# Attention scores in four 64x64 tiles of the array instead of two 64x128 tiles

## The chip, the cores and the metric

The kernel runs on one core of a Trainium2 chip. The metric is the device time of one execution in microseconds (us). Engines are named as in the profile: PE is TensorE (PEld its weight loads), DVE is VectorE, ACT is ScalarE, POOL is GpSimd and SP is SyncE, which here only issues DMAs.

## What is computed

The input is a batch of 16 images with 384 channels of 32 x 32 pixels. Two layers follow each other, each with a group normalisation (32 groups) before it and a residual after it: attention over the 1024 pixels of an image with 8 heads of 48 channels, and a depthwise convolution of 7 x 7. Cut to what matters:

```python
qkv = jnp.einsum('bnc,oc->bno', xt, w_qkv)
qkv = qkv.reshape(b, n, 3, NUM_HEADS, HEAD_DIM).transpose(2, 0, 3, 1, 4)
q, k, v = (qkv[0], qkv[1], qkv[2])
attn = jnp.einsum('bhnd,bhmd->bhnm', q, k) * SCALE
attn = jax.nn.softmax(attn, axis=-1)
out = jnp.einsum('bhnm,bhmd->bhnd', attn, v)
...
x = x + _L0_conv_ref(_gn(x), L0_conv_w_qkv, L0_conv_w_proj, L0_conv_b_proj)
x = x + _L1_conv_ref(_gn(x), L1_conv_weight)
```

All of it is in fp32.

## The kernel before, in words

The eight heads of an image are taken in four pairs, so there are 16 x 4 = 64 pairs, numbered u. A tile qks[u] holds the queries (index 0) and keys (index 1) of one pair for all 1024 pixels, with the channels on partitions: head 0 of the pair on partitions 0 to 47, head 1 on 64 to 111.

The scores of a pair are computed in 16 steps: two halves h of 512 queries, and in each of them eight blocks i of 128 keys. One step, s_step (L487), takes a score buffer in PSUM of 128 partitions (keys) x 2 heads x 512 queries, which is one PSUM bank for each head. It fills it with one product per head j: the stationary operand lhsT is 48 channels x 128 keys, the moving operand rhs 48 channels x 512 queries. The two heads lie on different rows of the array. Then ACT takes the exponential of the whole buffer into an SBUF tile e (L501). There are 16 x 64 = 1024 steps.

av_step (L503) multiplies the values with e: for each head a product with 128 keys x 64 columns as stationary operand (48 channels, a column of ones whose product is the sum of the softmax, and columns that aren't used) and 128 keys x 512 queries as moving operand. It accumulates over the eight blocks of keys into one PSUM bank, head 0 on partitions 0 to 63, head 1 on 64 to 127. take (L517) copies the bank out.

PSUM has three buffers of two banks that scores, queries and keys, values and projection share (ps_s), and two buffers of one bank (ps_o) for the accumulators. A score step therefore has to wait until the exponential three steps back has read its buffer.

The order of the work is written out by the program: the loop at the end of run() takes eight score steps in a row, then eight value steps (SIZES = [8] * 8, so an image has eight such groups), and between them the other stages for PE: queries and keys (qk_step, L435), values (v_step, L463) and the projection (proj_step, L555). A planner with estimated costs (clock for PE, vclock for DVE) decides where DVE's instructions stand: catch_up puts the taps of the depthwise convolution of an earlier image there (conv_tap, L636), and functions with a due time (after) such as divide, which divides by the softmax sums. act_slot does the same for ACT. The order of each engine's instructions is thus fixed when the program is built.

The convolution of three of the 48 channel tiles (128 channels of an image) is computed on PE at the end (conv_on_pe, L739): for each tap four products side by side, each with 128 rows x 32 columns of the array.

Of the kernel before, what the change touches and what calls it, by code (L numbers as in the profile page):

```python
# [16 lines left out]
P = 128  # L17
# [27 lines left out]
def kernel(  # L45
# [25 lines left out]
    nc = tc.nc  # L71
# [7 lines left out]
    HALF = N // 2  # L79
# [30 lines left out]
    def run(general):  # L110
        tag = "g" if general else "f"
        with ExitStack() as stack:
# [20 lines left out]
            def psum(name):  # L133
                return ps_s.tile([P, 2, HALF], F32, tag="s", name=name)

            xns, x1s, qks, os_, accs, es, xn1s = {}, {}, {}, {}, {}, {}, {}
# [350 lines left out]
            def s_step(n):  # L487

                u, h, i = n // (2 * NT), n // NT % 2, n % NT
                ps = psum(f"ps_s_{n}")  # L490
                for j in range(2):
                    r = slice(64 * j, 64 * j + D)
                    nc.tensor.matmul(  # L493
                        ps[:, j, :],
                        lhsT=qks[u][r, 1, i * P : (i + 1) * P],
                        rhs=qks[u][r, 0, h * HALF : (h + 1) * HALF],
                        start=True,
                        stop=True,
                    )
                es[n] = epool.tile([P, 2, HALF], F32, tag="e", name=f"e_{n}")  # L500
                nc.scalar.activation(es[n], ps, AF.Exp, scale=SCALE)  # L501

# [808 lines left out]
            for b, n0, size in [  # L1311
                (b, b * PER_B + sum(SIZES[:g]), SIZES[g]) for b in range(B) for g in range(len(SIZES))
            ]:
                r = n0 - b * PER_B
# [5 lines left out]
                for n in range(n0, n0 + size):  # L1320
                    s_step(n)
# [17 lines left out]
                for n in range(n0, n0 + size):  # L1339
                    av_step(n)  # L1340
                    u, h, i = n // (2 * NT), n // NT % 2, n % NT
# [102 lines left out]
```

## Time and profile before

| | us |
|---|---|
| median of 3 runs | 2908.01 (2907.54 to 2911.57) |
| span of the profiled execution, first to last instruction | 2904.5 |
| PE busy | 2894.4 |
| DVE busy | 2565.6 |
| ACT busy | 1461.4 |
| score matmuls (L493), busy | 914.2 |
| value matmuls (L509), busy | 907.2 |

In the rows of the profile a group is named by its line, engine, operation and tiles; "48*128" is the shape of the stationary operand (rows x columns of the array that are used), and "48x512 f32" that of the operand that streams or is loaded. After the shape come the count, the busy time in us (overlapping records counted once), the mean duration in ns, and the idle time of the engine before these instructions with what ended it. A product in fp32 is two weight loads and two matmuls in the records. Matmul records overlap, and a matmul's record is longer than the time by which it delays the next. Rows of a timeline give the start in us, the length in us, the engine, the line, the operation and how many records were merged.

The time around the span is 2908.0 - 2904.5 = 3.5 us. The clock of TensorE was 1.000 of full speed over the span. The DMA queues moved 175.80 MB, at a mean share of the DMA engines between 0 and 7 tenths in slices of 73 us.

### The profile page before, as it was taken

How to read it: one execution, taken by the hardware profiler on the slowest of the kernel's cores; microseconds unless marked ns; L12 is line 12 of the kernel's file. 1: busy time of each engine (PE TensorE's matmuls, PEld its weight loads, DVE VectorE, ACT ScalarE, POOL GpSimd, SP SyncE). 2: the span in 40 equal slices, each digit the busy share in tenths (PEclk: the TensorE clock that was granted, in tenths of full speed). 3: DMA queues.
4: the chain of work that ended last, by engine and by line, in shares of the span. 5: the costliest groups of instructions: out<-in, count | busy, mean ns of one | idle time of the engine just before them, and what ended most of it. 6: DMA issues, size and time to landing. Idle time of an engine off the chain costs nothing.

```text
span 2904.5 us, 30161 instructions
## 1 busy us (share of the span) xinstructions
PE 2894.4 (100%) x11446; PEld 1169.7 (40%) x11446; DVE 2565.6 (88%) x2559; ACT 1461.4 (50%) x1745; POOL 262.0 (9%) x411
## 2 busy tenths in 40 slices
PE   9999999999999999999999999999999999999999
PEld 4343343433434343343433434343343433434333
DVE  5313999989899898998989899898998989899997
ACT  2546445464453645545465454645545455454641
POOL 3111004010100101000010100101001010100101
PEclk9999999999999999999999999999999999999999
DMA  7422022220312203012120212213022130212346
GB/s 287 131 26 63 16 36 77 38 67 23 65 33 43 70 21 84 16 35 70 35 71 16 65 41 43 67 24 84 16 36 70 28 77 16 55 50 43 83 125 174
DMA packets 74284, 175.80 MB, mean 61 GB/s; under 512 B 30528, under 2 KB 32464, under 8 KB 72592
## 3 DMA queue, kind: packets, MB, share of 16 engines
q0 software_dynamic: 34336, 114.90, 15.9%
q1 hardware_dynamic: 38080, 55.20, 7.6%
q10 hardware_dynamic: 1712, 3.67, 0.4%
q8 instruction: 92, 1.51, 0.2%
q14 instruction: 64, 0.52, 0.1%
HBM read 118.61 MB, written 28.72 MB: 51 GB/s over the span
## 4 chain that ended last, share of the span: by engine, by line
PE 100%; DVE 0%; ACT 0%; POOL 0%; issue 0%; POOLq 0%
PE ps_s L493 31%; PE acc L509 31%; PE ps_qk L442 17%; PE ps_v L468 9%; PE ps_proj L562 8%; PE ps_conv L756 2%; PE ps_proj L599 1%; PE warm L1182 0%; PE ps_st_x L332 0%; PE ps_sum L588 0%; ACT qk L449 0%; POOL sc_x L353 0%; DVE x L360 0%; DVE x L777 0%; DVE ones_warm L1176 0%
## 5 line engine op out<-in xcount | busy, mean ns | idle before, releaser
L640 DVE SCALAR_TENSOR_TENSOR x<-xn,wsym,x 128x930 f32<-128x930 f32 (+9 forms) x2170 | 2363.9, 1172 | 138.8 <-ACT xn L364 138.7
L501 ACT ACTIVATE e<-ps_s 128x1024 f32<-128x1024 f32 x1024 | 952.5, 1051 | 54.5 <-PE ps_s L493 51.6
L493 PE MATMUL ps_s<-qk 48*128 48x512 f32 x4096 | 914.2, 596 | 1.1 <-ACT qk L449 1.1
L509 PE MATMUL acc<-e,v 128*64 128x512 f32 x4096 | 907.2, 595 | 0.0
L493 PEld LDWEIGHTS ps_s<-qk 48*128 48x128 f32 x4096 | 376.5, 185 | 535.0 <-ACT e L501 257.2
L509 PEld LDWEIGHTS acc<-e,v 128*64 128x64 f32 x4096 | 283.0, 137 | 608.2 <-issue 599.7
L442 PE MATMUL ps_qk<-x,wqk 128*128 128x512 f32 x1152 | 505.7, 595 | 1.0 <-DVE x L360 1.0
L520 ACT COPY o<-acc 128x512 f32<-128x512 f32 x128 | 75.2, 587 | 602.5 <-PE acc L509 602.3
L442 PEld LDWEIGHTS ps_qk<-x,wqk 128*128 128x128 f32 x1152 | 216.1, 190 | 287.1 <-issue 285.7
L468 PE MATMUL ps_v<-wv,x 128*128 128x384 f32 x768 | 252.0, 488 | 0.0
L562 PE MATMUL ps_proj<-o,wp 128*128 128x512 f32 x540 | 234.2, 592 | 0.0
L449 ACT COPY qk<-ps_qk 128x1024 f32<-128x1024 f32 x96 | 96.8, 1009 | 254.1 <-PE ps_qk L442 254.1
L577 POOL DMA_DIRECT2D x<-in_x x45 | 39.3, 872 | 1796.7 <-ACT x L570 1423.1
L468 PEld LDWEIGHTS ps_v<-wv,x 128*128 128x128 f32 x768 | 144.6, 190 | 109.7 <-ACT e L501 12.1
L562 PEld LDWEIGHTS ps_proj<-o,wp 128*128 128x128 f32 x540 | 102.6, 190 | 126.0 <-issue 120.3
L477 ACT COPY v<-ps_v 128x384 f32<-128x384 f32 x128 | 55.1, 483 | 185.6 <-PE ps_v L468 185.6
L570 ACT ACTIVATE x<-ps_proj,bp 128x1024 f32<-128x1024 f32 x45 | 50.2, 1115 | 182.7 <-PE ps_proj L562 182.7
L545 DVE TENSOR_TENSOR o<-o,inv 128x1024 f32<-128x1024 f32 x63 | 77.4, 1228 | 69.7 <-DMA inv<-inv 52.9
L364 ACT ACTIVATE xn<-x,sc_x 128x1024 f32<-128x1024 f32 x47 | 54.9, 1231 | 71.6 <-DMA sc_x<-gr_x 62.4
L756 PE MATMUL ps_conv<-sh,mat 128*32 128x480 f32 (+3 forms) x656 | 67.8, 569 | 0.0
L387 DVE BATCH_NORM_STATS2 bs_all<-xs 128x6 f32<-128x512 f32 x84 | 52.1, 682 | 17.3 <-DMA xs<-in_x 17.1
L458 POOL DMA_DIRECT2D qk<-qk x96 | 47.3, 526 | 116.4 <-ACT qk L449 115.4
(143 smaller groups left out, 565.4 us busy)
## 6 DMA issues: line engine op xcount, KB each, us to landing
x<-in_x POOLq DMA_DIRECT2D x90, 512.0 KB, 5.6
inv<-inv SPq DMA_DIRECT2D x126, 256.0 KB
out<-x POOLq DMA_DIRECT2D x45, 512.0 KB, 3.8
xs<-in_x POOLq DMA_DIRECT2D x42, 512.0 KB, 6.1
qk<-qk POOLq DMA_DIRECT2D x96, 128.0 KB, 5.9
o<-o SPq DMA_DIRECT2D x90, 64.0 KB
sh<-xd SPq DMA_DIRECT2D x32, 160.0 KB
x<-in_x SPq DMA_DIRECT2D x6, 512.0 KB
```

Of the source, the lines that this page charges most:

```text
L442: nc.tensor.matmul(ps[:, h, :], lhsT=wqk[:, k, s, t, :], rhs=xns[b][:, k, h * HALF : (h + 1) * HALF], start=(k == 0), stop=(k == NK - 1),)
L449: nc.scalar.copy(halves(qks[u][:, s, :]), ps)
L468: nc.tensor.matmul(ps[:, j, 0:C], lhsT=xns[b][:, k, t * P : (t + 1) * P], rhs=wv[:, k, :], start=(k == 0), stop=(k == NK - 1),)
L477: nc.scalar.copy(dst.rearrange("p (h d) -> p h d", d=D + 1)[:, :, 0:D], ps[:, j, 0:C].rearrange("p (h d) -> p h d", d=D),)
L493: nc.tensor.matmul(ps[:, j, :], lhsT=qks[u][r, 1, i * P : (i + 1) * P], rhs=qks[u][r, 0, h * HALF : (h + 1) * HALF], start=True, stop=True,)
L501: nc.scalar.activation(es[n], ps, AF.Exp, scale=SCALE)
L509: nc.tensor.matmul(accs[u, h][64 * j : 64 * j + 64, :], lhsT=v_of(u, i, j), rhs=e[:, j, :], start=(i == 0), stop=(i == NT - 1),)
L520: nc.scalar.copy(os_[u][:, h * HALF : (h + 1) * HALF], accs.pop((u, h)))
L545: nc.vector.tensor_tensor(os_[u], os_[u], invs.pop(u), ALU.mult)
L562: nc.tensor.matmul(ps[:, h, :], lhsT=wp[:, t, o * P : (o + 1) * P], rhs=os_[NP * b + t][:, h * HALF : (h + 1) * HALF], start=(t == 0), sto ...
L640: nc.vector.scalar_tensor_tensor(acc, xn1s[b, k].rearrange("p (h w) -> p h w", w=W)[:, iy, ix], wsym[:, k, dy + PAD, dx + PAD : dx + PAD + 1],
L756: nc.tensor.matmul(dst[CH * i : CH * (i + 1), :].rearrange("p (y x) -> p y x", x=W)[:, :, ox], lhsT=mats[k][:, i, d0 * KS + dx + PAD, :], ...
```

## The change

In s_step each head's product is split in two by keys: c = 0 takes the first 64 of the block's 128 keys and writes to partitions 0 to 63 of the score buffer, c = 1 takes the other 64 and writes to partitions 64 to 127. The queries are the same for both. The four products of a step lie on four different quarters of the array. The buffer, its contents, the exponential that reads it and everything else are as they were.

```diff
                 ps = psum(f"ps_s_{n}")
                 for j in range(2):
                     r = slice(64 * j, 64 * j + D)
-                    nc.tensor.matmul(
-                        ps[:, j, :],
-                        lhsT=qks[u][r, 1, i * P : (i + 1) * P],
-                        rhs=qks[u][r, 0, h * HALF : (h + 1) * HALF],
-                        start=True,
-                        stop=True,
-                    )
+                    for c in range(2):
+                        nc.tensor.matmul(
+                            ps[64 * c : 64 * c + 64, j, :],
+                            lhsT=qks[u][r, 1, i * P + 64 * c : i * P + 64 * c + 64],
+                            rhs=qks[u][r, 0, h * HALF : (h + 1) * HALF],
+                            start=True,
+                            stop=True,
+                        )
```

## The prediction

> **What bounds the kernel now.** I read the engine shares first, then the chain that ended last, then the costliest groups.
>
> ```profile
> PE 2894.4 (100%) x11446; PEld 1169.7 (40%) x11446; DVE 2565.6 (88%) x2559; ACT 1461.4 (50%) x1745; POOL 262.0 (9%) x411
> ...
> PE ps_s L493 31%; PE acc L509 31%; PE ps_qk L442 17%; PE ps_v L468 9%; PE ps_proj L562 8%; PE ps_conv L756 2%; PE ps_proj L599 1%; PE warm L1182 0%; PE ps_st_x L332 0%; PE ps_sum L588 0%; ACT qk L449 0%; POOL sc_x L353 0%; DVE x L360 0%; DVE x L777 0%; DVE ones_warm L1176 0%
> ...
> L501 ACT ACTIVATE e<-ps_s 128x1024 f32<-128x1024 f32 x1024 | 952.5, 1051 | 54.5 <-PE ps_s L493 51.6
> L493 PE MATMUL ps_s<-qk 48*128 48x512 f32 x4096 | 914.2, 596 | 1.1 <-ACT qk L449 1.1
> L509 PE MATMUL acc<-e,v 128*64 128x512 f32 x4096 | 907.2, 595 | 0.0
> L493 PEld LDWEIGHTS ps_s<-qk 48*128 48x128 f32 x4096 | 376.5, 185 | 535.0 <-ACT e L501 257.2
> ...
> L756 PE MATMUL ps_conv<-sh,mat 128*32 128x480 f32 (+3 forms) x656 | 67.8, 569 | 0.0
> ```
>
> PE is busy for the whole span and the chain never leaves it, so a nanosecond won or lost on PE in the score stage is one in the end. The score stage (L493) is 31% of the chain. 4096 matmul records over 1024 steps of two products are four records a step: each fp32 product is two weight loads and two matmuls, called pass a and pass b here. 914.2 us over 1024 steps is 893 ns for four matmuls of 589 ns: they overlap. How they overlap is in the timeline of the weight loads, at the turn into a score group and out of it, and at the start of the convolution on PE, which is the one place with four tiles at once:
>
> ```profile
> 1020.87 0.30 PEld L493 LDWEIGHTS ps_s<-qk 48*128 48x128 f32 x4 [0.76 <-issue]
> 1021.40 0.19 PEld L493 LDWEIGHTS ps_s<-qk 48*128 48x128 f32 x2 [0.23 <-issue]
> 1021.83 0.19 PEld L493 LDWEIGHTS ps_s<-qk 48*128 48x128 f32 x2 [0.23 <-issue]
> ...
> 1026.84 0.33 PEld L493 LDWEIGHTS ps_s<-qk 48*128 48x128 f32 x4 [0.53 <-ACT e L501]
> 1027.93 0.20 PEld L509 LDWEIGHTS acc<-e,v 128*64 128x64 f32 x4 [0.76 <-issue]
> 1028.41 0.14 PEld L509 LDWEIGHTS acc<-e,v 128*64 128x64 f32 x2 [0.28 <-issue]
> 1028.85 0.14 PEld L509 LDWEIGHTS acc<-e,v 128*64 128x64 f32 x2 [0.28 <-issue]
> ...
> 2826.91 0.16 PEld L756 LDWEIGHTS ps_conv<-sh,mat 128*32 128x32 f32 x8 [0.76 <-issue]
> 2827.37 0.13 PEld L756 LDWEIGHTS ps_conv<-sh,mat 128*32 128x32 f32 x4 [0.30 <-issue]
> 2827.80 0.13 PEld L756 LDWEIGHTS ps_conv<-sh,mat 128*32 128x32 f32 x4 [0.30 <-issue]
> ```
>
> A load starts when a matmul of its tile starts, so these rows count slots. In a slot of 0.43 us (1021.83 less 1021.40) all tiles run one pass side by side: two score tiles, two tiles of the second product (L509), four convolution tiles. A score step is two slots, 0.86 us. Three rows of the views by source line give the shortest, median and longest matmul:
>
> ```profile
> L493 PE MATMUL ps_s<-qk x4096: 589/589/693, 27.5 to 2796.5; 48*128 48x512 f32 x196
> L509 PE MATMUL acc<-e,v x4096: 592/592/645, 50.2 to 2814.8; 128*64 128x512 f32 x196
> L756 PE MATMUL ps_conv<-sh,mat x656: 551/565/617, 2826.9 to 2897.4; 128*32 128x480 f32 x48, 128*32 128x496 f32 x48, 128*32 128x464 f32 x47, 128*32 128x512 f32 x21
> ```
>
> The longest are the first of a group, which wait for their weights with nothing to cover the load: 104 ns more than the usual one with 128 columns, 53 with 64, 25 with 32 (617 less the 592 of the same 512 elements on L509). The timeline agrees: the first slot is 0.53 us in a score group and 0.48 in a group of L509.
>
> **What the Trainium skill says.** "TensorEngine Tiling (Array Packing)", Available Configurations, lists 64x64 as four tiles; Key Properties says that tiles work independently and that a change of tiling mode drains TensorE. The trace agrees on the drain: from the last matmul start of one stage (1020.34 of L442, 1027.41 of L493) to the first load of the next it is 0.53 and 0.52 us, against slots of 0.43, some 0.09 for each turn. "TensorE: Matmul & The Clock Gate", section LDWEIGHTS, says that a load takes as long as it has columns, whatever its rows, at 1.2 per ns; the 104, 53 and 25 ns above agree. Part 3 of that page gives 10.6 times for 16 tiles of 32x32, rows and columns split together; no stage of this kernel splits both, so the trace can't confirm it.
>
> **The change, part by part.** Removed from each step: four loads of 128 columns and four matmuls of 512 elements. Added: eight loads of 64 columns and eight matmuls of the same 512 elements, in four tiles. The elements streamed per tile don't change; the number of tiles does.
>
> 1. Steady slots. If four tiles overlap as two do, a step stays two slots of 429 ns: cost 0. What hides the doubled instruction count is the other tiles' streaming. The convolution is the nearest row: four loads and four matmuls a slot, for 45 us without a stop from 2851.8, at 390 to 429 ns a slot for 464 to 512 elements. The new score stage needs the same eight instructions every 429 ns, so issue should hold. The cover gone, each ns on a slot costs 1024 x 2 = 2.05 us.
> 2. First slot of a group. SIZES makes groups of 8 steps, 1024 / 8 = 128 groups. The exposed load shrinks from 128 to 64 columns: 533 to 480 ns, as on L509, a gain of 53 ns. Its bounds are 0 (the two column halves of a row pair load one after the other, two times 53) and 53. I take 53: on L509 two loads of 64 columns lie side by side (0.14 us for x2, each 0.137).
> 3. Skew. Tiles start one after another: x2 of 187 ns takes 0.19 us, x4 of 109 ns takes 0.13, so the last of two starts some 7 ns late and the last of four some 20. A group ends with its last tile, then drains: 14 ns more each. Bounds 0 and 14; I take 14.
> 4. Drain. 0.09 us in and out for all pairs of shapes that occur; I take no change, with 5 ns each way as bound, 2 x 128 x 5 = 1.3 us.
> 5. The wait for the score buffer. The first load of a step waits for the exponential that frees one of three buffers (257.2 us of PEld's idle time, nearly all covered). In the last step of a group that load starts at 1026.84 while the matmul running then began at 1026.55, so it has until 1026.98. Everything later on PE is queued behind it. A load half as long needs 53 ns less there, and the exponential starts 14 ns later: the slack grows. Few slots stall now (some 0.6 us in all, in three groups), so I count 0.
> 6. ACT, DVE, DMA. ACT (50%) has the same exponentials. DVE waits 138.7 us in 15 waits for the normalised next image, some 9 us an image, which depends on PE; PE coming 8 x 39 = 0.3 us earlier per image is absorbed there. No DMA is added or moved, on SP's or POOL's queue either; only 8192 more PE instructions are fetched, at a rate the convolution has already.
>
> Sum: 128 x (53 - 14) = 5.0 us less. The profiled span of 2904.5 becomes 2899.5; the median of the runs is 3.5 us above the span, which I keep: 2908.0 - 5.0 = 2903.0 us.
>
> **The rivals.**
>
> A, the forecast: four tiles overlap, and the short first load pays. With items 2 to 4 at their bounds the gain is 4.0 to 7.0 us: 2901.0 to 2904.0.
>
> B, loads of the two halves follow one another: no gain in item 2, the skew stays, 128 x 14 = 1.8 us more: 2909.8. For it: the two halves read the same 48 partitions, which no two loads of a group do now in a tile of fewer than 128 rows. Against: L509 loads two halves over all rows side by side.
>
> C, the slower side: the two column halves of a row pair stream the same query columns through the same rows, and get in each other's way. Place: every score slot. In full, halves take turns and a step has four slots: 1024 x 2 x 429 ns = 879 us more, some 3782. In part, a few ns on a slot: from 5.3 ns (to make up the 5.0 us and add 5.8) the kernel is slower by more than 0.2%, and at 6.3 ns it is at 2916. For it: no stage here splits rows and columns together, PE has nothing to cover a longer slot, and the convolution's slots carry 2 to 5 ns over their elements at 1.2 per ns. Against: L509 and L756 stream two and four tiles through the same rows without loss, L493 two through different rows.
>
> D, the turn gets cheaper, since L509 next to the scores has the same column split: half of 0.09 us saved on the way in gives 128 x 46 ns = 5.9 us more, 2897.1. Against: the turn costs 0.09 us also from L493 to L468, where only the row split changes.
>
> That the change doesn't do what it says would show as 4096 records on L493; the loop over c makes 8192.
>
> **How the numbers follow.** Differences of 0.2%, 5.8 us, are about what a measurement can tell from none, so the mark for faster is 2902.2, inside A's own range. A has 0.62: 0.29 of it beyond the mark (skew partly hidden, cheaper drain), 0.33 within. B has 0.07, within. D has 0.07, faster. C has 0.24, slower: 0.14 in full, 0.10 in part. So faster 0.36, same 0.40, slower 0.24. The range takes in A, B, D and most of the partial C, 2897 to 2916; about 0.16 is left out, nearly all of it C in full. A's own range is 2901.0 to 2904.0.
>
> **What would show it.** In the profile of the changed kernel: L493 with 8192 loads of 64 columns near 137 ns and 8192 matmuls at 589, longest near 642 (item 2; near 693 means B); load rows of x4 every 0.43 us (item 1; every 0.43 with x2 would be C in full); a score group of 7.02 to 7.03 us in the chain in place of 7.07; turns of 0.52 us. I am wrong if the slot is longer than 0.43, or if PE shows idle time behind the exponentials.

## The result and the profile after

The changed kernel takes 2902.51 us (median of 20 runs, 2900.85 to 2905.43), the kernel before in runs beside it 2909.84 us (20 runs, 2905.86 to 2911.73). The medians are 7.3 us apart. The ratio, worked out over the runs, is 0.9978, with a 95% interval of 0.9971 to 0.9984: 6.4 us less, between 4.7 and 8.4. A second set of runs, the first experiment below, gave 0.9980 (0.9973 to 0.9986), 5.8 us less. The gain is real and sits on the 0.2% mark. The forecast was 5.0 us less and 2903.0 us.

From the page of the changed kernel, whose score products are now L494 and value products L510: the shares, the chain and the costliest PE rows.

```profile
PE 2891.3 (100%) x15542; PEld 1084.1 (37%) x15542; DVE 2565.5 (88%) x2559; ACT 1461.0 (50%) x1745; POOL 262.8 (9%) x411
...
PE ps_s L494 31%; PE acc L510 31%; PE ps_qk L442 17%; PE ps_v L468 9%; PE ps_proj L563 8%; PE ps_conv L757 2%; PE ps_proj L600 1%; PE warm L1183 0%; PE ps_st_x L332 0%; PE ps_sum L589 0%; ACT qk L449 0%; DVE x L778 0%; DVE ones_warm L1177 0%
...
L494 PE MATMUL ps_s<-qk 48*64 48x512 f32 x8192 | 909.0, 592 | 1.1 <-ACT qk L449 1.1
L510 PE MATMUL acc<-e,v 128*64 128x512 f32 x4096 | 907.2, 595 | 0.0
L494 PEld LDWEIGHTS ps_s<-qk 48*64 48x64 f32 x8192 | 293.0, 132 | 606.4 <-ACT e L502 302.4
```

Twice as many score matmuls keep PE busy for 5.2 us less (914.2 before, 909.0 now), and the value products are where they were. PE still fills the span and the chain. The timeline of the weight loads shows where the 5.2 us are, at the same turn into a score group as before and at its end:

```profile
1020.61 0.21 PEld L494 LDWEIGHTS ps_s<-qk 48*64 48x64 f32 x8 [0.76 <-issue]
1021.10 0.15 PEld L494 LDWEIGHTS ps_s<-qk 48*64 48x64 f32 x4 [0.28 <-issue]
1021.52 0.15 PEld L494 LDWEIGHTS ps_s<-qk 48*64 48x64 f32 x4 [0.28 <-issue]
1021.95 0.15 PEld L494 LDWEIGHTS ps_s<-qk 48*64 48x64 f32 x4 [0.28 <-ACT qk L449]
...
1026.57 0.26 PEld L494 LDWEIGHTS ps_s<-qk 48*64 48x64 f32 x8 [0.60 <-ACT e L502]
1027.64 0.20 PEld L510 LDWEIGHTS acc<-e,v 128*64 128x64 f32 x4 [0.81 <-issue]
```

A slot still lasts 0.43 us (1021.95 less 1021.52), now with four loads in it: the four tiles run side by side. The first slot of the group is 0.48 to 0.49 us where it was 0.53. Four loads of 0.133 us take 0.15, so the last tile starts 20 ns after the first. From the start of the scores to the first load of L510 it is 7.03 us, against 7.06 before. The view by source line confirms the exposed load:

```profile
L494 PEld LDWEIGHTS ps_s<-qk x8192: 129/133/133, 29.0 to 2792.4; 48*64 48x64 f32 x200
L494 PE MATMUL ps_s<-qk x8192: 589/589/641, 29.0 to 2792.8; 48*64 48x512 f32 x200
```

The longest matmul is 52 ns above the median, as on the value products; it was 104. Taken over all 128 groups in the two traces, a group (first matmul to first matmul of the next stage) has a median of 7068 ns before and 7028 after, and all of them last 905.3 and 900.1 us.

The profiled spans are only 4.0 us apart, 2904.5 and 2900.5. From the first score matmul to the last it is 2769.0 us before (27.5 to 2796.5, in the prediction's row for L493) and 2763.8 after (29.0 to 2792.8), which is again 5.2 us. But in the second trace the first score matmul comes some 1.5 us later; 0.4 us come back behind the last one and were not followed further. Of the 1.5 us 1.2 lie in the warm-up matmuls of the first 10 us. The first row is the kernel before, the second the one after, each from a timeline of PE:

```profile
1.45 7.84 PE L1182 MATMUL warm<-ones_warm 128*128 128x384 f32 x18 [1.45 <-DVE ones_warm L1176]
```

```profile
1.46 9.13 PE L1183 MATMUL warm<-ones_warm 128*128 128x384 f32 x18 [1.46 <-DVE ones_warm L1177]
```

Nothing of the change is in these 18 matmuls. In the trace before, four of their slots last 640 ns and eleven 322; after, eight last 640 and seven 322. The clock was granted later in that execution, and from 14.5 to 17.9 us it was once more at 0.50, where it was 1.00 in the trace before. Runs of either kernel are spread over 4 to 6 us; the first experiment shows that the clock goes with this.

### The profile page after: what moved, and what is told of

The parts are those of the page before. It is cut to its first block, busy times and chain, and to the rows that moved or that the text cites. A ratio compares the mean times of both kernels' runs of the same rounds, so it can differ in the third digit from the quotient of the medians.

```text
span 2900.5 us, 38353 instructions
## 1 busy us (share of the span) xinstructions
PE 2891.3 (100%) x15542; PEld 1084.1 (37%) x15542; DVE 2565.5 (88%) x2559; ACT 1461.0 (50%) x1745; POOL 262.8 (9%) x411
## 4 chain that ended last, share of the span: by engine, by line
PE 100%; DVE 0%; ACT 0%; issue 0%
PE ps_s L494 31%; PE acc L510 31%; PE ps_qk L442 17%; PE ps_v L468 9%; PE ps_proj L563 8%; PE ps_conv L757 2%; PE ps_proj L600 1%; PE warm L1183 0%; PE ps_st_x L332 0%; PE ps_sum L589 0%; ACT qk L449 0%; DVE x L778 0%; DVE ones_warm L1177 0%
## 5 line engine op out<-in xcount | busy, mean ns | idle before, releaser
L494 PE MATMUL ps_s<-qk 48*64 48x512 f32 x8192 | 909.0, 592 | 1.1 <-ACT qk L449 1.1
L510 PE MATMUL acc<-e,v 128*64 128x512 f32 x4096 | 907.2, 595 | 0.0
L494 PEld LDWEIGHTS ps_s<-qk 48*64 48x64 f32 x8192 | 293.0, 132 | 606.4 <-ACT e L502 302.4
L510 PEld LDWEIGHTS acc<-e,v 128*64 128x64 f32 x4096 | 282.7, 137 | 614.5 <-issue 605.4
L757 PE MATMUL ps_conv<-sh,mat 128*32 128x464 f32 (+3 forms) x656 | 67.3, 569 | 0.0
L535 DVE RECIPROCAL rec<-sums 128x16 f32<-128x16 f32 x63 | 15.4, 244 | 49.3 <-DMA sums<-sum 49.3
```

The source lines that it names most:

```text
L494: nc.tensor.matmul(ps[64 * c : 64 * c + 64, j, :], lhsT=qks[u][r, 1, i * P + 64 * c : i * P + 64 * c + 64], rhs=qks[u][r, 0, h * HALF : (h ...
L510: nc.tensor.matmul(accs[u, h][64 * j : 64 * j + 64, :], lhsT=v_of(u, i, j), rhs=e[:, j, :], start=(i == 0), stop=(i == NT - 1),)
L757: nc.tensor.matmul(dst[CH * i : CH * (i + 1), :].rearrange("p (y x) -> p y x", x=W)[:, :, ox], lhsT=mats[k][:, i, d0 * KS + dx + PAD, :], ...
```

## The experiments

Each ratio is to the kernel before, run beside it on the same chip. Line numbers shift by a few from kernel to kernel.

**The changed kernel again.**

> The changed kernel once more, beside the kernel before, for the size of the gain and for the spans of both. Theory (the first load of each of the 128 score groups is exposed for 53 ns less, less 13 ns of skew at its end, nothing else): 5.2 us less, ratio 0.9982, and the total time of the score groups from their first matmul to the next stage falls from 905.3 to 900.1 us. Rival (there is a second gain of about 2 us elsewhere, since the medians of the first result lie 7 us apart): ratio 0.9975 or below, and some other stage is shorter in every profile.

Measured: 2902.32 us against 2908.47, ratio 0.9980 (0.9973 to 0.9986). Score groups 900.8 us in all, with one group 0.7 us long, where ACT was late with an exponential; the median is again 7028 ns. No other stage is shorter. In the stages of PE the 40 ns for each group are the only gain that the traces show. That the medians lie 6 to 7 us apart rather than 5.2 is inside the interval, and part of it goes with the clock: runs with a mean clock of 1.000, 0.999 and 0.998 have medians of 2906.6, 2907.9 and 2909.2 us in the kernel before, and of 2900.9, 2902.3 and 2903.7 in the changed one. At equal clock it is 5.5 to 5.8 us less. No second gain was found.

**Eight tiles a step.** The edit to the changed kernel:

```diff
-                    for c in range(2):
+                    for c in range(4):
                         nc.tensor.matmul(
-                            ps[64 * c : 64 * c + 64, j, :],
-                            lhsT=qks[u][r, 1, i * P + 64 * c : i * P + 64 * c + 64],
+                            ps[32 * c : 32 * c + 32, j, :],
+                            lhsT=qks[u][r, 1, i * P + 32 * c : i * P + 32 * c + 32],
```

> Each score step as eight products of 32 keys in 64x32 tiles. Theory of load less skew: the exposed load falls to some 25 ns, first slot 453 ns; the last of eight tiles starts 7 x 6.7 = 47 ns after the first, so a group lasts as long as with four tiles (27 less, 27 more): same time as the changed kernel within 1 us, ratio to before 0.998. Rival, issue: sixteen instructions have to start every 429 ns, 27 ns each, where the convolution showed 49; if 49 were the limit a slot would last 784 ns and the kernel take some 730 us more. Rival, loads of one row group follow one another: first slot 0.53 us.

Measured: 2911.14 us, ratio 1.0010 (1.0001 to 1.0018), against the expectation. Yet the median group is 7028 ns, to the nanosecond that of four tiles: first slot 453, last of eight tiles 47 ns late, slots of 429. The theory of a group held and its sum over the kernel did not. All 13 runs (2907.27 to 2915.19) lie above all 21 of the repeat of the changed kernel (2900.78 to 2904.02), and in the one that was profiled the loss is at one place. In windows of the eight-tile run (length; busy time and count of PE, PEld, DVE, ACT and POOL; granted clock, DMA share, GB/s):

```profile
176.00:180.00 4.00, 4.00 (x78) 1.29 (x62) 0.74 (x1) 3.37 (x4) 0.00 (x0) 1.00 0.10 4
180.00:184.00 4.00, 0.99 (x10) 0.29 (x7) 0.00 (x0) 0.00 (x0) 0.00 (x0) 1.00 0.00 0
184.00:190.00 6.00, 6.00 (x30) 1.19 (x25) 0.00 (x0) 3.08 (x4) 0.00 (x0) 0.53 0.00 0
```

and in its timelines of PEld and PE:

```profile
183.55 0.13 PEld L494 LDWEIGHTS ps_s<-qk 48*32 48x32 f32 x2 [3.91 <-issue]
```

```profile
183.56 5.07 PE L494 MATMUL ps_s<-qk 48*32 48x512 f32 x26 [3.01 <-issue]
```

PE stood still for 3 to 4 us in the middle of a score group, with no semaphore to wait for ("issue"), and then worked at a clock of 0.53 until past 190 us. That one group is 7.2 us longer than the median and the value group behind it 1.3: 8.5 of the 8.6 us by which the span (2909.5) exceeds that of the repeat above (2900.9). What was under way is in the DMA records: the queue that brings instructions moves 16 KB at a time, usually in 1.1 us; the packet of 178.9 us took 6.6, and no other packet moved meanwhile. From 183.55 us the loads came back a few at a time, and a full step of sixteen at 186.44, 1.0 us after the packet's end at 185.4. The queue's packets rise from 92 before to 124 with four tiles and 188 with eight, for 8192 and another 16384 instructions of PE: 256 to a packet. By an estimate from this and the slots, eight tiles use a packet up in 6.9 us (27 ns each) and four in 13.7 (54 ns each), so a fetch of 6.6 us leaves eight tiles next to nothing. Why it took so long is open.

**Eight tiles, but not yet in the first two images.**

```diff
-                    for c in range(4):
+                    m = 64 if n < 2 * PER_B else 32
+                    for c in range(P // m):
...
```

> Eight tiles of 64x32 for a score step as before, but only from the third image on; the first two images in four 64x64 tiles. In the run with eight tiles PE stood still at 180 us while a fetch of instructions took 6.6 us. Theory (that one event, in a time with late instruction fetches, made it slower): no standstill, the kernel takes what the changed one takes within 1.5 us, ratio 0.998. Rival (eight tiles cost something in every group or at many places): 5 us or more above the changed kernel, ratio 1.000 or more.

Measured: 2904.16 us (2902.13 to 2906.34), ratio 0.9981 (0.9973 to 0.9989). There is no standstill; the score groups have a median of 7027 ns and last 900.7 us in all. A fetch of instructions at 176.6 us took 9.5 us in this run, and one of 7.9 us at 176.3 is in the changed kernel too. Of the 13 profiles 11 have one of 6.5 to 11.0 us near 175 us (the kernel before has 3.3 us, the next experiment 2.6), and only with sixteen instructions in a slot at that time did PE stand still. So the standstill goes with the number of instructions there, and in a group eight tiles cost nothing more than four. That the late fetch is its cause is inferred from the times above; the fetch itself was not changed alone.

**Four tiles only in the first step of a group.**

```diff
-                    for c in range(2):
+                    m = 64 if n % 8 == 0 else P
+                    for c in range(P // m):
...
```

> Only the first of the eight steps of a group in four 64x64 tiles, the other seven in two 64x128 tiles. Theory that any change of tile shape is a turn (drain of 0.09 us, then an exposed load of 104 ns): against before each group gains 53 ns and loses about 0.2 us, 128 x 0.15 = 19 us slower, ratio 1.006 to 1.007. Rival (only a change of the row split drains, tiles of one row split mix freely): the short first load without the skew at the end, 128 x 53 ns = 6.8 us faster than before, 1.6 us faster than the changed kernel, ratio 0.9977.

Measured: 2928.91 us, ratio 1.0076 (1.0062 to 1.0090): the theory. The median group is 7228 ns, 160 more than before. The timeline of its weight loads shows two turns where there was one:

```profile
1029.21 0.21 PEld L495 LDWEIGHTS ps_s<-qk 48*64 48x64 f32 x8 [0.76 <-issue]
1030.23 0.30 PEld L495 LDWEIGHTS ps_s<-qk 48*128 48x128 f32 x4 [0.81 <-issue]
1030.77 0.19 PEld L495 LDWEIGHTS ps_s<-qk 48*128 48x128 f32 x2 [0.24 <-issue]
1031.20 0.19 PEld L495 LDWEIGHTS ps_s<-qk 48*128 48x128 f32 x2 [0.23 <-issue]
```

The first step takes 1.02 us up to the next load: a first slot of 0.48, a second of 0.43, 0.02 of skew and 0.09 of drain. Then the 64x128 tiles pay their own first slot of 0.54. Tiles with the same row split don't mix for free: what the Trainium skill says of a change of mode ("TensorEngine Tiling (Array Packing)", Key Properties) holds within one stage too.

**Groups of four steps, before and after.** In the kernel before and in the changed one:

```diff
-            SIZES = [8] * 8
+            SIZES = [4] * 16
```

> The kernel before with groups of 4 steps in place of 8, so 256 score groups. Theory: each extra score group costs a turn in (some 0.09 us and 104 ns) and each extra group of value products one (0.09 and 53 ns), 128 x 0.34 = 43 us slower than before, ratio 1.015. It is the base for the next run; no rival is told apart by it alone.

> The changed kernel with groups of 4 steps. Theory (the gain is 40 ns for each group): 256 x 40 = 10.2 us less than the run before it with groups of 4, and the median score group is 40 ns shorter in the profiles. Rival (the gain is not tied to the start of a group, but to the steps, to the exponentials' waits or to the ends of the kernel): 5 to 7 us less, as with groups of 8.

Measured: 2962.64 us (ratio 1.0182, 1.0168 to 1.0195) and 2957.47 us (1.0161, 1.0148 to 1.0175). The first is 10 us above what was expected: some 7 us are one long score group at 2748 us (below) and the value group behind it, 3 us are turns of values and projection, which now stand next to value products. The median score group is 3634 and 3594 ns: 40 ns again, now in 256 groups, 10.2 us. The times differ by 5.2 us only, which looks like the rival. It isn't: the gain per group was there, and the profiles show where most of the rest was lost, the larger part at one place near the end. From the waits of PE, two tiles first, then four:

```profile
PE ps_s L493 <- ACT e L501: 5.1, 2, 4.8
```

```profile
PE ps_s L494 <- ACT e L502: 6.8, 1, 6.8
```

and from the timeline of the four-tile run at that place:

```profile
2740.50 0.61 POOL L274 DMA_DIRECT2D gr_x<-af_x  x1 [10.12 <-DVE af_x L315]
2744.68 0.78 POOL L278 DMA_DIRECT2D sc_x<-gr_x  x1 [3.56 <-DMA gr_x<-af_x]
...
2746.99 3.50 ACT L364 ACTIVATE xn<-x,sc_x 128x1024 f32<-128x1024 f32 x3 [7.43 <-DMA sc_x<-gr_x]
...
2751.46 1.99 PE L494 MATMUL ps_s<-qk 48*64 48x512 f32 x8 [6.83 <-ACT e L502]
```

The scale factors of an image come late from DVE (af_x), two DMAs follow each other, ACT's normalisation waits for them, and the exponentials queue behind it in ACT's order. With four tiles PE arrives 6.4 us earlier and the exponentials start 4.3 us earlier, so it waits 2.0 us longer. The score and value groups at this place take 3.1 us more than in the run with two tiles, also because the clock was at half for 10.2 us around this wait, in the other run for 6.8. Another 1.5 us are in the first queries and keys, at 16.9 us, where the clock was at 0.51 from 13.3 to 20.2 us in this profile. The times agree as far as they go: of the runs with a mean clock of 0.999, the one with four tiles took 2953.42 us and the two with two tiles 2960.99 and 2961.26. With groups of eight this place has no such wait.

**Value products in four tiles of 32 columns.**

```diff
-                    nc.tensor.matmul(
-                        accs[u, h][64 * j : 64 * j + 64, :],
-                        lhsT=v_of(u, i, j),
+                    for c in range(2):
+                        nc.tensor.matmul(
+                            accs[u, h][64 * j + 32 * c : 64 * j + 32 * c + 32, :],
+                            lhsT=v_of(u, i, j)[:, 32 * c : 32 * c + 32],
...
```

> The changed kernel, with the value products in four tiles of 32 columns too. Theory of load less skew: first slot of a value group 453 in place of 480 ns, skew at its end 20 in place of 7 ns: a value group is 14 ns shorter, 128 x 14 = 1.8 us less than the changed kernel, at the edge of what the times can tell, but plain in the profile (median group 7018 to 7004 ns). Rival (instructions are late when there are more of them, as in the run with eight tiles): some groups are us longer, and the time is above the changed kernel's.

Measured: 2902.61 us, ratio 0.9982 (0.9975 to 0.9989). The median value group fell from 7018 to 7004 ns, as worked out, and all value groups from 898.3 to 896.9 us; one of them, at 182.6 us, while a fetch of 9.9 us was under way, is 0.33 us longer than the rest. In the times the 1.4 us can't be seen.

**64 columns in every stage.** Queries and keys, values and projection of the changed kernel get the same edit; for queries and keys:

```diff
-                        nc.tensor.matmul(
-                            ps[:, h, :],
-                            lhsT=wqk[:, k, s, t, :],
+                        for c in range(2):
+                            r = slice(64 * c, 64 * c + 64)
+                            nc.tensor.matmul(
+                                ps[r, h, :],
+                                lhsT=wqk[:, k, s, t, r],
...
```

> The changed kernel with queries, keys, values and projection in two tiles of 64 columns too, so that they have the tile shape of the value products. Theory that the shape makes the turn: the 32 turns from value products to queries and keys (0.09 us of drain and 104 ns of exposed load each) and the 15 back (0.09 and 53) vanish, and 16 first slots of values shorten by 51 ns: 6.3 + 2.2 + 0.8 = 9.3 us less than the changed kernel, ratio to before 0.995. Rival (a turn is paid at a change of stage whatever the shape): only the exposed loads shorten, 48 x 51 ns and 16 x 51 ns, some 3 us less than the changed kernel, ratio 0.997.

> All stages with 64 columns once more, for a tighter interval and a second profile. Theory: around 2897 us, ratio 0.9965, and most likely a profile with PE idle for some us near 180 us. Rival (the first five runs were high by chance): 2893 to 2895 us.

Measured: 2897.55 us (ratio 0.9966, 0.9952 to 0.9979) and, the second time, 2896.53 us (0.9957, 0.9943 to 0.9970). The turn is gone where the shapes agree. In the timeline of PE of the first run:

```profile
1008.17 0.60 PE L513 MATMUL acc<-e,v 128*64 128x512 f32 x2
1008.60 1.03 PE L444 MATMUL ps_qk<-x,wqk 128*64 128x512 f32 x4
```

From the last value products to the first queries it is 0.43 us, a plain slot, where it was 0.52; and a stage of queries and keys has a median of 10400 ns for 10497. Queries and keys, values and value products together last 9.8 us less than in the repeat of the changed kernel (1641.7 for 1651.6 us). The times show 5 to 6, between the theory and the rival; it is the trace that decides for the theory. The standstill near 180 us that was expected of most executions is in neither profile. The second one shows something else, the longest wait of PE:

```profile
PE ps_proj L604 <- DVE o L596: 2.3, 1, 2.3
```

At 2812 us, in the last image, the projection waits for the last division by the softmax sums, which stands behind taps of the convolution in DVE's queue. In the changed kernel the slot of the projection at this division lasts 617 ns, 0.08 us more than in the kernel before (535) and in the first profile here (534).

Why DVE was late in one execution of the same kernel and not in the other can be read from the two profiles. From the division of another pair, at 2760.06 us in the first and 2761.75 in the second, DVE works down its queue for some 46.6 us to the last one. Before that division it stood idle for 1.9 us in the first and 4.4 in the second, and the DMA that brings the inverse sums to it (inv<-inv) was issued 1.5 and 4.1 us after the one that has to land before it (inv<-rec). So the wait at 2812 us points to a late DMA, passed on through a queue with only 0.5 us of room left: for so long DVE waits for PE at the last division in the first profile.

**The first two images with full tiles.** In the three stages of the run before, for values:

```diff
-                        for c in range(2):
+                        m = P if b < 2 else 64
+                        for c in range(P // m):
                             nc.tensor.matmul(
-                                ps[64 * c : 64 * c + 64, j, 0:C],
-                                lhsT=xns[b][:, k, t * P + 64 * c : t * P + 64 * c + 64],
+                                ps[m * c : m * c + m, j, 0:C],
+                                lhsT=xns[b][:, k, t * P + m * c : t * P + m * c + m],
...
```

> As the run with 64 columns in all stages, but queries, keys, values and projection of the first two images in full 128-column tiles. By the totals of the PE stages all-64 was 10.0 us below the changed kernel, by its times only some 5. Theory (most of its executions lose 2 to 3 us to a late instruction fetch near 180 us, as eight tiles did; its profile is one that didn't): with fewer instructions in the first images no execution loses it; 14 of 16 images keep 8.7 us, so 2893 to 2894 us, ratio 0.995. Rival (the difference is lost elsewhere, in waits for exponentials or at the start): no better than all-64, 2897 us or more.

Measured: 2898.37 us (2892.85 to 2902.76), ratio 0.9958 (0.9945 to 0.9972), no better. The theory of the late fetch falls for this kernel: its profile, taken of its longest run, has no standstill near 180 us, and PE waits 4.4 us for DVE at the last division and then works at half clock for six slots of 0.85 us. Here the DMA inv<-inv was issued 6.9 us after inv<-rec. The rival's "elsewhere" is this wait in the execution that was profiled; the shortest run, 10 us below that one, has no profile.

**Room for DVE.** All stages with 64 columns, and in the planner:

```diff
-                    vclock += 4.2
+                    vclock += 7.2
```

> All stages with 64 columns, and the planner told that DVE has 3.0 us less time around the last division (4.2 becomes 7.2), so that two taps of the convolution stand behind that division instead of before it. In the second profile of all-64 PE waited 2.3 us there for DVE, at 2812 us; in the first one and in the changed kernel it waited less than 0.3 us. Theory (with PE earlier, DVE's queue before that division is what is late): the wait goes, 1 to 3 us less than all-64 in the times, 2894 to 2895.5 us, ratio 0.995. Rival (the two taps come back on the path to the end): no gain, 2896 to 2897 us.

Measured: 2894.38 us (2892.66 to 2895.76), ratio 0.9952 (0.9938 to 0.9966), the fastest of all versions. In the trace it is one tap and one addition of the same width that now stand behind the division. PE's wait for it is gone from the list of its waits, DVE waits 2.1 us for PE there instead, and the profiled span is 2890.5 us. The DMA of the inverse sums was not late in this execution (1.5 us), so the profile shows the room, but not that a late DMA is now covered. The range of its times overlaps with those of the other two all-64 runs; that it is faster than they are is likely, not certain.

## Why the prediction was right

1. Steady slots, cost 0: right. 429 ns before and after, with eight instructions in each instead of four. The convolution's rows were the right witness, and the eight-tile run shows that sixteen fit as well, as long as they have been fetched.
2. First slot, gain 53 ns: right. 533 to 480 ns in all 128 groups, the longest matmul 641 for 693. So the two halves of a row pair load side by side, and rival B is out: its longest matmul would have stayed near 693.
3. Skew, cost 14 ns: right. 20 ns at the end of a group for 6.6. The eight-tile run, 27 ns less at the start and 27 more at the end for the same 7028 ns, shows that the two terms make up the group's time.
4. Drain, no change: right. 519 ns out of a score group and 522 in, from matmul start to matmul start, as before. So rival D is out: 64x64 and the 128x64 of L509 have the same column split, and the turn between them costs the same. The run with mixed tiles in a group shows it for shapes that have the same row split.
5. The wait for the score buffer, cost 0: right. More idle time of PEld ends with an exponential (302.4 us for 257.2), because the loads themselves are shorter (293.0 us for 376.5). PE's own waits show nothing of it, and the four longest score groups exceed the median by 0.55 us in all, by 0.63 before.
6. Other engines, cost 0: right for this change and close to its limit. The first sign of DVE's limit is the 0.08 us at the last division. With 9 to 10 us gained on PE it took 2 and 4 us back in two of the three profiles without the added room for DVE, those in which a DMA ahead of it was late.

The sum of 5.0 us met 5.2 in the traces. Rival C, in full or in part, would have lengthened the slots and is excluded. Two things were off. The 3.5 us around the span were taken as the median less the span of another execution. Each run of the two kernels with both numbers has 2.1 to 2.3 us around the span, so the profiled execution of the kernel before was one of some 2906.6 us; it cancels in the difference. And the range given for A does not follow from the bounds named for it: with the 53 ns kept, the skew between 0 and 14 ns and the drain at plus or minus 1.3 us, the gain is 3.7 to 8.1 us, not 4.0 to 7.0. The traces lie inside both.

That the median, 2902.5 us, fell only 0.5 us from the forecast's 2903.0 is in part luck. The three runs that the forecast started from have a median 1.8 us below that of the twenty (2908.0 and 2909.8), and the medians are 7.3 us apart where 5.0 were forecast; the two nearly cancel. What the traces confirm is the 40 ns for each group.

The forecast put the time on the side of "same" by 0.8 us and gave faster almost the same chance. At a mark of 5.8 us, measured gains of 6.4 and 5.8 with intervals of some 2 us to either side don't decide between the two.

## What to carry to other kernels

Where PE never waits, read its stages as slots: a slot lasted as long as its operand streamed, with two, four or eight tiles alike, and what a stage's beginning cost here was a drain, paid when the tile shape changes, and a first weight load that nothing covers, paid by its columns. Narrower tiles shorten that load and add a few ns of skew for each tile at the end, so four here were as good as eight; giving neighbouring stages one shape saved more PE time (some 9 of the 9.8 us) than narrowing one of them (5.2), though the times kept only 5 to 6 of it. Look for what the gain runs into: here a DVE queue before the last division that has no room for a late DMA, ACT's order behind late scale factors, and a PE that runs out of fetched instructions.

## What the runs showed of the hardware

- Rows and columns split together ran four and eight fp32 tiles side by side without loss: slots of 429 ns with 4, 8 and 16 instructions in them, down to 27 ns for each.
- A turn cost some 90 to 94 ns of drain between any two shapes of the stages here, 64x64 to 64x128 included, and nothing between two stages of one shape (422 ns from the last start of one to the first of the next for tiles of 64 columns; 429 from projection to queries in the kernel before, both 128x128).
- PE can run dry. With 27 ns for each instruction it was idle for 3 to 4 us during a fetch of 6.6 us, and it came back at a clock of 0.53; the whole event cost 8.5 us. At 54 ns for each instruction fetches of 7.9 and 9.5 us left no trace.
